# A graph layer with attention as host for its messages: layer changes, gather lead and the b2 add rearranged

## Chip, cores and metric

One Trainium2 chip, one core. The metric is the device time of one execution in microseconds (us), the median of several runs. All data is fp32.

## What is computed

One layer of a graph transformer on 3125 nodes of 256 features and 100,000 directed edges with three attributes each: a graph convolution and a four-layer transformer over the same normalized nodes, added, then a mixture of experts. Cut to what matters:

```
xn = layernorm(x)
# graph convolution
m   = concat([xn[src], edge_attr], 1)
h_N = segment_sum(relu(m @ W1.T + b1), dst, N)
h   = relu(concat([xn, h_N], 1) @ W2.T);  h = h / max(norm(h), 1e-12)
# transformer, 4 layers, 8 heads, no mask
for i in range(4):
    z = layernorm(y) * g1[i] + c1[i]
    q = softmax(z @ Wq[i] * s, over the head's 32 features)
    k = softmax(z @ Wk[i] * s, over the nodes)
    y = y + (q @ (k.T @ (z @ Wv[i])) per head) @ Wo[i] + bo[i]
    z = layernorm(y) * g2[i] + c2[i]
    y = y + gelu(z @ W1[i] + b1[i]) @ W2[i] + b2[i]
x = x + h + y
# 16 experts, the two best of each node, their shares by softmax
x = x + layernorm(moe(layernorm(x)) + layernorm(x)) * gamma + beta
```

## The kernel before

The nodes lie in 25 tiles of 125. The transformer takes them in seven blocks (`BLOCKS`) of 4, 4, 4, 4, 4, 3 and 2 tiles, numbered 0 to 6; blocks of more than two tiles are worked in pairs of tiles.

**Engines and order.** Instructions of PE, ACT and POOL go out in the order in which the code stands; so do those of DVE inside the `manual_schedule` blocks. Elsewhere a scheduler arranges DVE.

**Messages.** The message product over node features is done once per node (`proj`, in DRAM). `load_chunk` (L338) gathers 128 rows of `proj` by an indirect DMA from POOL's queue. Eight chunks make a group, of which there are 98; a group's rows lie in two of six `gat` buffers, and its edge attributes come by SP's queue into one of two `ea` buffers. `message_step` (L383) multiplies the attributes by their weights on PE (`pw`), adds the product to the gathered rows on DVE (L397), applies relu on ACT (L398) and builds a one-hot matrix `hot` on DVE (L400). A group later, `sum_step` (L358) runs `sum_pq` (L372), 16 products of `hot` and `gat` into `pq` and a copy to `osb` on ACT (L381), and, for the group before that, `sum_win` (L362): two transposes of `osb` and four adds into `hNT` on DVE.

**Where they run.** The groups are spread as filler through layers 0 to 2. The list `due` (L407) gives each step a place, in groups: a chunk of group g at g + 0.125 (j + 1) - LEAD for its j-th (from 0), with LEAD 1.25; the sum step at g; the message step at g + 0.5. `worked` (L426) is called by each stage of the transformer with the columns that it put on PE, moves `place` on by a share of the total, and issues the steps that have come due. Ahead of the first gather of such a call POOL copies one element of what the stage made (`tick`, L436), so that gathers can't run ahead of the transformer. `held` keeps `worked` from issuing anything; `only_loads` limits it to gathers.

**A layer.** For each block b the loop (L860) does: first FFN product with gelu (`stage_f1`); exponential keys and q transposed (`stage_ek`, `stage_qT`) and the key-value product (`stage_m`) of the next layer's block b - 2; attention output (`stage_y`) of block b + 1; the transposed first norm (`stage_t1`) of block b - 1; second norm (`stage_ln2`) of b + 1; the second FFN product (`stage_f2`); keys and q (`stage_k`, `stage_q`) of b - 1 for the next layer; and so on. `stage_ln2` also adds b2 to the block's residual, by `add_b2` (L714), on POOL.

**The layer change.** `stage_m` sums keys times values over all blocks (`msum`), rescaled when the running maximum of the keys grows; so the next attention output can't begin before the last block's keys are done. After the last second FFN product come k and q of block 5, its `ek`, `hT` of block 6, halves of m of block 5 with k of block 6 between them, q transposes of 5, `ek` of 6 and m of 6. `context` (L642) then divides by the key sums (`mean`), starts the last block's q, transposes (`meanT`), multiplies by Wv (`ctx`, kept per head in `ctxT`) and Wo (`mo`), with the shares of the last q between. Its argument `between` lists what PE is given at three points. After it the y products start. Message steps run here too: `fill(2)` (L440) issues one message step after the last FFN product, `fill_win` (L448) starts one sum step after `ek` of block 6, and the rest of it (`sum_pq`) is given to `context` or, at the change to the last layer, runs at once where there is one.

**After the messages.** From 1604 us the last layer runs without them, with the products of the graph convolution (`stage_g`, called `h` in the convolution's formula) as filler in its context and b2 added block by block; the experts follow.

Of the kernel before, what the change touches and what calls it, by code (L numbers as in the profile page):

```python
# [8 lines left out]
F32 = mybir.dt.float32  # L9
# [8 lines left out]
D = 256  # L18
P = 128
TP = 125  # L20
# [5 lines left out]
NG = (NCH + G - 1) // G  # L26
# [13 lines left out]
BT = 4  # L40
# [25 lines left out]
def gps_layer(ctx: ExitStack, tc: tile.TileContext, a, out):  # L66
# [153 lines left out]
    with ExitStack() as ph:  # L220
# [205 lines left out]
        def worked(columns, mark=None):  # L426
# [6 lines left out]
            while due and due[-1][0] <= place and not (only_loads and due[-1][1]):  # L433
# [158 lines left out]
        def q_shares(pair, qf):  # L592
# [49 lines left out]
        def context(l, between):  # L642
# [60 lines left out]

        def stage_ln2(b, adder=nc.gpsimd):
            r = BLOCKS[b]
            finish_stats(r)
            xh = tmp.tile([TP, BT, D], F32, name="xh")
            st["xh", b] = xh
            for i, t in enumerate(r):
                normalize(xh[:, i, :], xm[:, t, :], t)  # L710
            if adder is not None:
                add_b2(b, adder)

        def add_b2(b, adder=nc.gpsimd):  # L714
            r = BLOCKS[b]
            xs = xm[:, r[0]:r[-1] + 1, :]
            adder.tensor_add(xs, xs, b2[:TP, None, :].to_broadcast([TP, len(r), D]))
# [86 lines left out]

        rest = None
        in_order = {mybir.EngineType.PE, mybir.EngineType.Activation, mybir.EngineType.Pool}
        last = DEPTH - 1
        with tc.manual_schedule(engines=in_order):

# [7 lines left out]
            for b in range(NB):  # L817
# [3 lines left out]
                if b < NB - 1:  # L821
                    stage_q(0, b)
                else:
                    held = True
                if b > 1:
# [19 lines left out]
            stage_m(0, NB - 1)  # L845
            for l in range(last):
                start_layer(l)
                with tc.manual_schedule(engines={mybir.EngineType.DVE}):
                    if l == 0:
                        context(l, [lambda: stage_qT(l, NB - 2, slice(0, 1)),  # L850
                                    lambda: stage_qT(l, NB - 2, slice(1, 2)), lambda: None])
                    else:
                        context(l, [lambda: None, lambda: None, rest])
                    load(l + 1, "Wk", "Wq", "Wv")
                    (y00, y01), (y10, y11), (y20, y21) = [pairs(b) for b in range(3)]
                    y_added(*y_products(y00))
                    held, only_loads = False, True
                    y_added(*y_products(y01))
                    stage_ln2(0, None)
# [5 lines left out]
                    y21 = y_products(y21)  # L865
                    for y in (y11, y20, y21):
                        y_added(*y)
                    only_loads = False
                for b in range(NB):
# [12 lines left out]
                    if b + 1 < NB:  # L882
                        stage_ln2(b + 1)
                    stage_f2(l, b)
                    stage_stats(b)
# [6 lines left out]
                    if b + 1 < NB:  # L892
                        stage_t2(l, b + 1)
                    if b > 0:
                        stage_q(l + 1, b - 1)
                    if b < NB - 1:
                        stage_ln1(b)
                stage_ek(l + 1, NB - 2)
                stage_t1(l + 1, NB - 1)
                stage_m(l + 1, NB - 2, [0])  # L900
                stage_k(l + 1, NB - 1)
                stage_m(l + 1, NB - 2, [1])
                stage_qT(l + 1, NB - 2)
                stage_ek(l + 1, NB - 1)
                rest = fill_win()
                if l + 1 == last:
                    rest()
                stage_m(l + 1, NB - 1)
            while due:
                _, _, step, i = due.pop()  # L910
                step(i)
# [296 lines left out]
        with tc.manual_schedule(engines=in_order - {mybir.EngineType.Pool}):  # L1208
# [7 lines left out]
            with tc.manual_schedule(engines={mybir.EngineType.DVE}):  # L1216
                context(last, [lambda: stage_g(0, slice(0, 1)), lambda: stage_g(0, slice(1, 2)),
                               lambda: stage_qT(last, NB - 1)])
# [279 lines left out]
```

## Time and profile before

The median of five runs is 2163.39 us (2153.59 to 2173.75).

| | |
|---|---|
| profiled execution, its time | 2163.46 us |
| its span | 2161.8 us |
| mean granted clock of PE over the span | 0.932 |
| first and last message add on DVE (L397) | 161.5 and 1551.4 us |
| last second FFN product to first y product, layer 0 to 1 | 602.98 to 635.73 us |
| the same, 1 to 2 | 1091.22 to 1123.58 us |
| the same, 2 to 3 | 1571.05 to 1603.65 us |
| gathers on POOL (L348) | 784, 969 ns each, 760.1 us busy |

The profile is of one execution. PE is TensorE's products, PEld its weight loads, DVE VectorE, ACT ScalarE, POOL GpSimd; a queue that starts DMAs has a q behind its engine's name. A line such as `L397 DVE TENSOR_TENSOR gat<-gat,pw` names the code line, the engine, the operation, what is written and what is read. "idle before" is the time for which an engine did nothing ahead of an instruction, and the name after the arrow is what ended it, where the profile can tell: "issue" means nothing that it shows, "remote" an event of another queue. The granted clock is the part of full speed at which PE was let run.

### The profile page before, as it was taken

To read this page: it belongs to the slowest core of one execution; us is meant where nothing else is said; L and a number is where in the kernel's file an instruction comes from. 1 tells how busy PE (TensorE), PEld (TensorE's weight loads), DVE (VectorE), ACT (ScalarE), POOL (GpSimd) and SP (SyncE) were. 2 spreads that over 40 slices of the span, in tenths; PEclk is the share of its full clock that TensorE was granted. 3 is DMA by queue.
4 is the path that set the end of the run, shared out by engine and by line. 5 is a ranking of instruction groups with operands and counts; after the bars stand their busy time and mean duration, and the time that the engine had idled before them with its cause. 6 is when DMAs were issued, how large, how long until landed. Compare 5 with 4: busy or idle time off the path is not lost. (4 is left out here: it accounts for less than half of the span.)

```text
span 2161.8 us, 28580 instructions
## 1 busy us (share of the span) xinstructions
PE 1916.7 (89%) x8965; PEld 1262.8 (58%) x8965; DVE 1167.3 (54%) x3729; ACT 748.5 (35%) x1352; POOL 1110.8 (51%) x1404
## 2 busy tenths in 40 slices
PE   6997998898888989898888998898889999899984
PEld 4774554554564554555564454555676777778761
DVE  8654454645565455555565546555565566533335
ACT  3532334334323344344433334343422222222222
POOL 1016666666627666566626656666303335655431
PEclk9998999998888989898999989999999999999997
DMA  6122222232322222223322222332222101477846
GB/s 180 58 68 84 85 78 86 76 86 82 100 82 83 81 83 86 74 84 87 109 85 79 83 75 79 86 86 81 73 81 73 42 18 29 131 265 269 275 170 178
DMA packets 95088, 216.64 MB, mean 100 GB/s; under 512 B 26760, under 2 KB 53391, under 8 KB 90192
## 3 DMA queue, kind: packets, MB, share of 16 engines
q0 software_dynamic: 45904, 121.36, 19.5%
q1 hardware_dynamic: 49024, 93.34, 13.5%
q8 instruction: 77, 1.26, 0.2%
q14 instruction: 83, 0.68, 0.1%
HBM read 192.20 MB, written 22.35 MB: 99 GB/s over the span
## 5 line engine op out<-in xcount | busy, mean ns | idle before, releaser
L348 POOL DMA_INDIRECT gat<-proj,src_i x784 | 760.1, 969 | 229.1 <-issue 188.6
L745 PE MATMUL f_ps<-ww,gT 128*125 128x256 f32 x1600 | 378.9, 391 | 14.5 <-issue 9.1
L735 PE MATMUL f_ps<-h2T,ww 128*128 128x500 f32 (+2 forms) x896 | 376.8, 570 | 16.7 <-ACT h2T L459 6.6
L745 PEld LDWEIGHTS f_ps<-ww,gT 128*125 128x125 f32 x1600 | 300.5, 192 | 93.9 <-issue 33.9
L397 DVE TENSOR_TENSOR gat<-gat,pw 128x512 f32<-128x512 f32 x392 | 251.9, 678 | 153.6 <-PE pw L392 91.4
L398 ACT ACTIVATE gat<-gat 128x512 f32<-128x512 f32 x392 | 238.4, 630 | 276.7 <-DVE gat L397 183.6
L735 PEld LDWEIGHTS f_ps<-h2T,ww 128*128 128x128 f32 x896 | 172.2, 199 | 200.1 <-issue 138.7
L737 ACT ACTIVATE gT<-f_ps,ffb 128x500 f32<-128x500 f32 (+2 forms) x224 | 135.9, 631 | 139.2 <-PE f_ps L735 108.1
L392 PE MATMUL pw<-w1w,ea 8*128 8x512 f32 x784 | 147.2, 662 | 32.6 <-issue 5.8
L378 PE MATMUL pq<-gat,hot 128*32 128x256 f32 x1568 | 149.2, 399 | 30.1 <-ACT gat L398 20.2
L370 DVE TENSOR_TENSOR hNT<-hNT,win_ps 128x64 f32 x392 | 84.8, 216 | 132.7 <-remote 45.7
L381 ACT COPY osb<-pq 128x256 f32<-128x256 f32 x98 | 36.5, 372 | 324.1 <-remote 149.7
L400 DVE TENSOR_TENSOR hot<-slot,drel 128x256 f32<-128x256 f32 x98 | 49.0, 500 | 157.5 <-remote 58.2
L688 PE MATMUL y_ps<-mo,qT 128*125 128x256 f32 x400 | 107.3, 418 | 11.7 <-issue 5.0
L576 PE MATMUL q_ps<-wwq,hT 128*125 128x256 f32 x400 | 107.0, 423 | 9.7 <-DVE gat L397 7.8
L1201 POOL DMA_INDIRECT slots<-rec,at x50 | 59.5, 1189 | 105.5 <-DVE rs_u L115 63.7
L750 DVE TENSOR_TENSOR xm<-xm,f_ps 125x512 f32<-125x512 f32 (+1 forms) x52 | 34.6, 666 | 139.2 <-PE f_ps L745 69.0
L629 PE MATMUL m_ps<-xh,ek 125*128 125x257 f32 x400 | 101.2, 402 | 9.5 <-issue 5.2
L378 PEld LDWEIGHTS pq<-gat,hot 128*32 128x32 f32 x1568 | 52.2, 111 | 95.8 <-issue 43.5
L552 PE MATMUL k_ps<-hT,wwk 128*128 128x500 f32 (+2 forms) x224 | 102.1, 604 | 5.1 <-DVE hT L461 4.4
L576 PEld LDWEIGHTS q_ps<-wwq,hT 128*125 128x125 f32 x400 | 82.5, 212 | 36.4 <-DVE gat L397 10.8
L688 PEld LDWEIGHTS y_ps<-mo,qT 128*125 128x125 f32 x400 | 80.4, 207 | 37.0 <-issue 11.6
(270 smaller groups left out, 2673.6 us busy)
## 6 DMA issues: line engine op xcount, KB each, us to landing
ew<-ffn_w SPq DMA_DIRECT2D x33, 1154.0 KB
gat<-proj,src_i POOLq DMA_INDIRECT x784
ww<-mix_W SPq DMA_DIRECT2D x8, 1024.0 KB
ea<-ea_g SPq DMA_DIRECT2D x98, 64.0 KB
hNT<-ffn_w SPq DMA_DIRECT2D x4, 1154.0 KB
ogs<-outs SPq DMA_DIRECT2D x10, 448.0 KB
xnT_d<-stage SPq DMA_DIRECT2D x5, 500.0 KB
xnT<-xnT_d SPq DMA_DIRECT2D x5, 500.0 KB
```

Of the source, the lines that this page charges most:

```text
L348: nc.gpsimd.indirect_dma_start(out=gats[-1][:, (j // SC) % 2, j % SC, :], out_offset=None, in_=proj, in_offset=bass.IndirectOffsetOnAxis(a ...
L378: nc.tensor.matmul(pq[s * W:(s + 1) * W, :], hot[:, s * SC + i, :], gats[s // 2][:, s % 2, i, :], start=(i == 0), stop=(i == SC - 1))
L392: nc.tensor.matmul(pws[s], ea[s * W:s * W + SC * 4, :], w1w[s * W:s * W + SC * 4, :], start=True, stop=True)
L397: nc.vector.tensor_add(msg, msg, pws[s])
L398: nc.scalar.activation(msg, msg, AF.Relu)
L552: nc.tensor.matmul(ps, wt["Wk"][:, h, c * P:(c + 1) * P], hT[:, h, :m], start=(h == 0), stop=(h == KC - 1))
L576: nc.tensor.matmul(ps[:, i, :], st["hT", b][:, c, cols(o + i)], wt["Wq"][:, c, :], start=(c == 0), stop=(c == KC - 1))
L629: nc.tensor.matmul(ps, st["ek", b][:, i, c * P:(c + 1) * P], xh1s[b % 2][:, i, :], start=(i == 0), stop=(i == n - 1))
L688: nc.tensor.matmul(ps[:, i, :], qT[:, c, cols(t0 + i)], mo[:, c, :], start=(c == 0), stop=(c == KC - 1))
L735: nc.tensor.matmul(ps, wt["W1"][:, c, f * P:(f + 1) * P], st["h2T", b][:, c, :m], start=(c == 0), stop=(c == KC - 1))
L737: nc.scalar.activation(gT[:, f, :m], ps, AF.Gelu, bias=ffb[:, l, f:f + 1])
L745: nc.tensor.matmul(ps[:, i, :], st["gT", b][:, f, cols(o + i)], wt["W2"][:, f, :], start=(f == 0), stop=(f == NF - 1))
```

## The change

- LEAD goes from 1.25 to 1.5: gathers and loads of attributes are issued a quarter of a group earlier.
- The sum step of group g is due at g + 0.15 instead of g. The message step stays at g + 0.5.
- `fill` and its call are gone, so no message step is issued in a layer change. `fill_win` and the rest of its sum step are offered in `context` for layers 1 and 2 alone, between `meanT` and `ctx` and between `ctx` and `mo`; in the instructions as built it finds no sum step to start there.
- The last block's q is made ahead of m of that block, by the new `last_q`, in a buffer of the tag "xh"; the shares stay in `context`. The q transposes of block 5 move to the start of `context`, ahead of `meanT`; those of block 6 from between the y products to the end of `context`. The four lists of `between` are called at four points instead of three.
- In the layer change, k of block 5 now stands ahead of the first norm of block 6; the shares of block 5 stand after both of its exponentials.
- DVE's order is that of the code from the statistics of the last block through the y products of the next layer, where before it was so from `context` on.
- b2 is added on DVE in layers 0 to 2 (7 adds a layer, 21 in all). In the last layer it stays on POOL, except for the one that was on DVE before.

```diff
-        LEAD = 1.25
+        LEAD = 1.5
         due = [(c / G + 1 / G - LEAD, 0, load_chunk, c) for c in range(NCP)]
-        due += [(g, 1, sum_step, g) for g in range(1, NG + 2)]
+        due += [(g + 0.15, 1, sum_step, g) for g in range(1, NG + 2)]
         due += [(g + 0.5, 2, message_step, g) for g in range(NG)]
...
-        def fill(kind):
-
-            while due and due[-1][1] in (0, kind):
-                _, k, step, i = due.pop()
-                step(i)
-                if k == kind:
-                    return
...
+        def last_q(b):
+
+            st["qs", b] = tmp.tile([TP, BT, D], F32, tag="xh", name="qs")
+            pair, = pairs(b)
+            st["q", b] = pair, q_exp(b, pair, q_products(b, pair))[0]
...
             for c in range(KC):
                 nc.vector.tensor_scalar(mean[:, c, :], msum[:, c, :D], ksr[:, c:c + 1], None, op0=ALU.mult)
-
-            b = NB - 1
-            pair, = pairs(b)
-            st["qs", b] = tmp.tile([TP, BT, D], F32, name="qs")
-            q_ps = q_products(b, pair)
+            between[0]()
...
             affine(meanT, ps, l, 0)
-            qf, _ = q_exp(b, pair, q_ps)
-            between[0]()
+            between[1]()
...
             nc.vector.tensor_mul(ctxT, ps, bmask[:, None, :].to_broadcast([P, KC, P]))
-            q_shares(pair, qf)
-            between[1]()
+            q_shares(*st["q", NB - 1])
+            between[2]()
...
-            between[2]()
+            between[3]()
...
-        def stage_ln2(b, adder=nc.gpsimd):
+        def stage_ln2(b, adder=nc.vector):
...
-        def add_b2(b, adder=nc.gpsimd):
+        def add_b2(b, adder=nc.vector):
...
+                context(l, [lambda: stage_qT(l, NB - 2), sums_begun, lambda: rest[0](),
+                            lambda: stage_qT(l, NB - 1)])
...
-                    y10, y11 = y_products(y10), y_products(y11)
-                    stage_qT(l, NB - 1)
-                    y20 = y_products(y20)
-                    y_added(*y10)
-                    stage_t2(l, 0)
...
+                y10, y11, y20 = y_products(y10), y_products(y11), y_products(y20)
+                y_added(*y10)
+                stage_t2(l, 0)
...
+                dve.close()
...
-                    if b == NB - 1:
-                        stage_ln1(b)
-                        held = True
-                        fill(2)
...
+                held = True
+                dve = dve_in_order()
+                stage_stats(NB - 1)
+                stage_k(l + 1, NB - 2)
+                stage_ln1(NB - 1)
+                st["qs", NB - 2] = tmp.tile([TP, BT, D], F32, name="qs")
+                two = [(pair, q_products(NB - 2, pair)) for pair in pairs(NB - 2)]
+                qfs = [(two[0][0], q_exp(NB - 2, *two[0])[0])]
                 stage_ek(l + 1, NB - 2)
                 stage_t1(l + 1, NB - 1)
+                qfs += [(two[1][0], q_exp(NB - 2, *two[1])[0])]
+                for pair_qf in qfs:
+                    q_shares(*pair_qf)
                 stage_m(l + 1, NB - 2, [0])
                 stage_k(l + 1, NB - 1)
+                last_q(NB - 1)
+                stage_ek(l + 1, NB - 1)
                 stage_m(l + 1, NB - 2, [1])
-                stage_qT(l + 1, NB - 2)
-                stage_ek(l + 1, NB - 1)
-                rest = fill_win()
-                if l + 1 == last:
-                    rest()
                 stage_m(l + 1, NB - 1)
+            dve.close()
...
-                        add_b2(0)
+                        add_b2(0, nc.gpsimd)
```

More of the change, by code (lines that the diff above doesn't have):

```diff
@@ L803, in start_layer, with dve_in_order @@
             nc.sync.dma_start(b2, rows_bcast(a["mix_b2"][l], P))
-        rest = None
         in_order = {mybir.EngineType.PE, mybir.EngineType.Activation, mybir.EngineType.Pool}
         last = DEPTH - 1
+        def dve_in_order():
+            stack = ExitStack()
+            stack.enter_context(tc.manual_schedule(engines={mybir.EngineType.DVE}))
+            return stack
         with tc.manual_schedule(engines=in_order):
@@ L823, in gps_layer @@
                 else:
+                    last_q(b)
                     held = True
@@ L846, in gps_layer, with sums_begun @@
             for l in range(last):
+                if l == 0:
+                    dve = dve_in_order()
                 start_layer(l)
[L848 to L859, printed above, removed]
-                    y10, y11 = y_products(y10), y_products(y11)
-                    stage_qT(l, NB - 1)
-                    y20 = y_products(y20)
-                    y_added(*y10)
-                    stage_t2(l, 0)
[L865 to L868, printed above, removed]
+                rest = [lambda: None]
+                def sums_begun():
+                    if l > 0:
+                        rest[0] = fill_win()
+                context(l, [lambda: stage_qT(l, NB - 2), sums_begun, lambda: rest[0](),
+                            lambda: stage_qT(l, NB - 1)])
+                load(l + 1, "Wk", "Wq", "Wv")
+                (y00, y01), (y10, y11), (y20, y21) = [pairs(b) for b in range(3)]
+                y_added(*y_products(y00))
+                held, only_loads = False, True
+                y_added(*y_products(y01))
+                stage_ln2(0, None)
+                y10, y11, y20 = y_products(y10), y_products(y11), y_products(y20)
+                y_added(*y10)
+                stage_t2(l, 0)
+                y21 = y_products(y21)
+                for y in (y11, y20, y21):
+                    y_added(*y)
+                only_loads = False
+                dve.close()
                 for b in range(NB):
@@ L884, in gps_layer @@
                     stage_f2(l, b)
+                    if b == NB - 1:
+                        break
                     stage_stats(b)
[L886 to L889 removed]
                     if b > 0:
                         stage_k(l + 1, b - 1)
[L892 to L893 removed]
+                    stage_t2(l, b + 1)
                     if b > 0:
                         stage_q(l + 1, b - 1)
[L896 to L897 removed]
+                    stage_ln1(b)
+                held = True
+                dve = dve_in_order()
+                stage_stats(NB - 1)
[4 more added lines that the diff above has]
+                qfs = [(two[0][0], q_exp(NB - 2, *two[0])[0])]
                 stage_ek(l + 1, NB - 2)
                 stage_t1(l + 1, NB - 1)
+                qfs += [(two[1][0], q_exp(NB - 2, *two[1])[0])]
+                for pair_qf in qfs:
+                    q_shares(*pair_qf)
                 stage_m(l + 1, NB - 2, [0])
                 stage_k(l + 1, NB - 1)
+                last_q(NB - 1)
+                stage_ek(l + 1, NB - 1)
                 stage_m(l + 1, NB - 2, [1])
[L903 to L907 removed]
                 stage_m(l + 1, NB - 1)
+            dve.close()
             while due:
@@ L1216, in gps_layer @@
             with tc.manual_schedule(engines={mybir.EngineType.DVE}):
-                context(last, [lambda: stage_g(0, slice(0, 1)), lambda: stage_g(0, slice(1, 2)),
-                               lambda: stage_qT(last, NB - 1)])
+                context(last, [lambda: stage_qT(last, NB - 2), lambda: stage_g(0, slice(0, 1)),
+                               lambda: stage_g(0, slice(1, 2)), lambda: stage_qT(last, NB - 1)])
                 stage_y(last, 0)
```

## The prediction

> **What bounds the kernel now.** I read the totals and slices first, then a table of stretches, then the list of waits, then the timeline of one layer change.
>
> The totals and slices give the engine that sets the end:
>
> ```profile
> PE 1916.7 (89%) x8965; PEld 1262.8 (58%) x8965; DVE 1167.3 (54%) x3729; ACT 748.5 (35%) x1352; POOL 1110.8 (51%) x1404
> ...
> PE   6997998898888989898888998898889999899984
> ...
> PEclk9998999998888989898999989999999999999997
> ```
>
> PE is busy 89% of 2161.8 us, and its slices fall to 8 only where DVE, ACT and POOL work too; there the granted clock falls as well. The stretches say how much this is (columns after the length: busy time of PE, weight load, DVE, ACT, POOL; granted clock; DMA share; GB/s). The first three are the steady parts of layers 0, 1 and 2, the next three the changes of layer, the last is layer 3 after the messages:
>
> ```profile
> 145.00:602.00 457.00, 396.83 (x1926) 237.91 (x1925) 238.26 (x716) 169.67 (x296) 296.75 (x405) 0.91 0.29 83
> 636.00:1092.00 456.00, 409.41 (x1958) 241.52 (x1961) 242.53 (x727) 173.20 (x301) 293.65 (x397) 0.92 0.29 84
> 1124.00:1570.00 446.00, 399.93 (x1908) 237.46 (x1907) 242.71 (x714) 167.45 (x292) 266.37 (x359) 0.93 0.27 78
> 602.98:636.00 33.02, 25.83 (x119) 18.98 (x120) 22.21 (x65) 11.26 (x23) 7.68 (x9) 0.84 0.34 97
> 1092.00:1124.00 32.00, 25.50 (x129) 18.44 (x121) 22.11 (x69) 11.34 (x23) 9.80 (x11) 0.89 0.37 110
> 1570.00:1604.00 34.00, 27.98 (x135) 22.93 (x134) 20.12 (x69) 9.79 (x20) 0.00 (x0) 1.00 0.37 113
> 1604.00:1822.00 218.00, 218.00 (x925) 164.63 (x924) 132.72 (x591) 57.25 (x88) 72.32 (x55) 1.00 0.15 39
> ```
>
> Without messages PE is full at clock 1.00. In the steady parts it idles 60.2 + 46.6 + 46.1 = 153 us, and the missing 9, 8 and 7% of clock are worth at most 41 + 36 + 31 = 108 us: some 0.7 us of lost clock beside each idle us. Idle time of PE in the steady parts is thus what can be won, and the waits between 145 and 1570 us name it (sum, times, longest, in us):
>
> ```profile
> ACT gat L398 <- DMA gat<-proj,src_i: 27.2, 13, 6.4
> PE pq L378 <- ACT gat L398: 20.2, 18, 2.6
> DVE gat L397 <- DMA gat<-proj,src_i: 17.9, 8, 5.5
> ```
>
> PE's largest single wait is that of the sums `pq` for the relu of the messages of their own group; the messages themselves wait for gathered rows. PE's waits for `gat` on DVE, ahead of second-norm transposes, q products and window transposes, are 8.2 + 7.8 + 3.9 = 19.9 us more. A change of layer looks like this (start, length, engine, what; in brackets the idle time before):
>
> ```profile
> 610.36 0.54 DVE L554 TENSOR_REDUCE here<-k_ps 128x1 f32<-128x375 f32 x1
> ...
> 611.75 0.54 DVE L554 TENSOR_REDUCE here<-k_ps 128x1 f32<-128x375 f32 x1
> ```
> ```profile
> 613.36 1.89 PE L614 MATMUL ek_ps<-ident,ekT 128*125 128x128 f32 x6 [3.99 <-ACT ekT L563]
> ```
>
> The message adds and the rsqrt steps stand ahead of and between the two maxima of the keys; PE waits 3.99 us for the exponentials, and from 612.3 to 622.5 its clock is 0.50.
>
> **Part 1: layer changes, A = -2 us.** From the last FFN product to the first y product they take 32.75, 32.36 and 32.60 us. Message steps fill 2.59 us of PE in the first (window transposes, sums, edge products) and 3.97 in the second; these move to the steady part at the same PE cost, so the net changes are 30.16 and 28.39. After the change: the wait of 3.06 us for the exponentials in the second goes (four message adds of 0.68 left DVE ahead of the maxima); m of the last block comes to wait some 1.85 us, since in the order by hand DVE reaches its keys' maxima only after the shares of two pairs of q (1.00 + 0.32 + 1.03 = 2.35 us in the second change, of which I let 0.5 lie beside other work); and the last block's q transposes (0.59) move ahead of y. 28.39 - 3.06 + 1.85 + 0.59 = 27.8, for the first and second change: -2.4 and -0.6. At 2-3, where no message step runs and no wait exceeds 1.6 us, only the additions apply: +2.4. The q transposes leave the y phase twice (-1.2); the first context gains 0.4, as the last q is ready before it. Sum -2.2, taken as -2. Bounds: if none of the added waits appears and the half clock of the first change (8.46 us of work at 0.5, 4.2 lost) goes too, -12; if DVE's order written by hand waits at each step for ACT as it does once for `meanT` (1.43 us in the second change), some six more steps across three changes make +8. The gathers that were pulled in there are issued later, with the others; they cost POOL 0.97 us each wherever they run.
>
> **Part 2: sums 0.15 group later, B = -10.** Groups follow each other every 14.3 us (first message add at 161.5, last at 1551.4, 97 intervals): 0.15 is 2.15 us. That is over the mean of the 18 waits of `pq`, 20.2 / 18 = 1.12, and just under the longest, 2.6. All 20.2 us could go; but PE then meets the next late result earlier, so I take half. Bounds 0 and -20.2. Late next are `osb` and the window transposes of the same sum, which follow a group later and so have cover.
>
> **Part 3: gathers 0.25 group earlier, C = -5.** 3.6 us against waits for gathered rows of up to 5.5 and 6.4, 45.1 in all. Only what reaches PE counts: 19.9 us for `gat` on DVE; I take a quarter, since those adds also wait for `pw` (91.4 us on DVE). Bounds 0 and -18. The cost: `gat` has six buffers, three groups. The first gather of group g is due at g - 1.125 and comes to g - 1.375; the sums that free its buffer, those of g - 3, were due at g - 2 and come to g - 1.85. The slack shrinks from 0.875 to 0.475 group, 12.5 to 6.8 us. On POOL's queue all later gathers and the `tick` copies are behind a gather that waits; for `ea` on SP's queue, with two buffers freed by the edge products, it shrinks from 0.375 to 0.125 group, 1.8 us, with later loads behind it.
>
> **Part 4: b2 on DVE, D = +3.** The rows:
>
> ```profile
> L717 POOL TENSOR_TENSOR xm<-xm,b x27: 1277/2357/2382, 184.7 to 1795.1; 125x1024 f32<-125x1024 f32 x20, 125x768 f32<-125x768 f32 x4, 125x512 f32<-125x512 f32 x3
> ```
> ```profile
> L1423 DVE TENSOR_TENSOR ogs<-ogs,gamma 125x1024 f32<-125x1024 f32 x5 | 6.1, 1225 | 1.0 <-ACT ogs L1418 1.0
> ```
> ```profile
> L400 DVE TENSOR_TENSOR hot<-slot,drel x98: 390/425/3094, 122.4 to 1536.0; 128x256 f32<-128x256 f32 x98
> ```
>
> On DVE a layer's adds take 5 x 1.225 + 0.95 (768 columns, between the rows) + 0.69 (its one row of 512) = 7.77 us, 23.3 in three layers. DVE is 53% busy there, so I let its idle half hide 12; behind each add on DVE's queue stand message adds, FFN evictions and `finish_stats`, for which PE waits, so 11 are left. Back come 7.7 us, what four `hot` comparisons of 2.2 to 3.1 us took above their 0.42 beside L717 on POOL. 11 - 8 = +3. Bounds: 0 and, with the cover gone, +23.3. POOL is relieved of some 45 us, which it need not have: the page has it 51% busy.
>
> The Trainium skill, GPSIMD Engine Reference, section 1 (Specifications), has GpSimd and VectorE share their SBUF interfaces, with contention for DVE instructions with two SBUF inputs; the b2 add is one, and it now runs beside gathers issued by POOL, which speaks against this part. The trace shows the contention beside the POOL add (`hot`, 3.09 us for 0.42), but not beside gathers: the shares of q, with two SBUF inputs too, never take over 695 ns in 52. If the rule held there as beside L717, 21 adds at seven times their price would cost 23.3 x 6 = 140 us more; by the row nothing.
>
> **Part 5: clock, E = -4.** A to D take -2 - 10 - 5 + 3 = -14 of idle time from PE; at 0.7 that would bring -10. The waits that go are short, 1 to 3 us, where the throttle shown above followed 3.99, so I take -4, 0.3 for each us (0 to -10).
>
> **Sum.** -2 - 10 - 5 + 3 - 4 = -18, against the profiled execution's 2163.46 (span 2161.8, 1.7 around it), 0.07 above the median 2163.39: 2145.5, forecast 2146.
>
> **Rivals.** First: nothing measurable. The sums' waits only move to the next product, since the groups' pace is set by DVE and ACT; A and D remain, 2163.5 - 2 + 3 = 2164. For it: 183.6 us of ACT's idle time ends with DVE's message adds. Against: `pq` waits on that relu directly, and a wait shorter than the delay can't stay. Second: slower, DVE becomes the bound. Place: the FFN of each steady part, where a b2 add ahead of an eviction holds the PSUM that PE needs. All 23.3 us exposed, no gain from B and C, and 0.3 of it more by the clock as in part 5 (7): 2163.5 - 2 + 30 = 2192. It decides once over half of the adds' time is exposed and B fails. For it: PE's waits ended by DVE between 145 and 1570 us come to some 56 us already. Against: DVE is idle 47% of the steady parts, and PE's other 97 us of idle time there are not ended by it. Third: the earlier gathers find no free buffers, since POOL waits for the sums three groups back, which became later; then C is lost, 2151. For it: `osb` copies that come up to 10.5 us after their sums, more than 6.8 of slack.
>
> **How the numbers follow.** Forecast 0.50 (own range 2130 to 2160), nothing measurable 0.22, DVE the bound 0.18, no free buffers 0.10. A measurement here tells 0.5% from no change: 10.8 us, so faster is below 2152.6, slower above 2174.2. Faster: 0.42 of the forecast, 0.06 of the third rival, 0.02 of the first: 0.50. Slower: 0.17 of the second, 0.03 of the first: 0.20. Same: 0.30. The range takes most of the second rival's lower half and, below, B and C near their full bounds with D at 3: 2163.5 - 2 - 20 - 18 + 3 - 10 = 2116; 2115 to 2182.
>
> **What would show it.** Right, step by step: the wait of `pq` for the relu falls below 8 us; waits for gathered rows fall below 20; L717 is on DVE near 1.2 us in layers 0 to 2, and no `hot` exceeds 1 us beside it; the clock stays at 1.00 in the layer changes, which last 27 to 29 us; the steady parts get shorter by 4 to 6 us each. Wrong: PE's waits for DVE rise above 56 us, POOL waits for `pq` ahead of gathers, or the clock in the steady parts falls below 0.91.

## The result, and the profile after

The change makes the kernel a little slower: 2171.19 us (median of 52 runs) against 2163.72 (94 runs), a ratio of 1.0023 with a 95% interval of [1.0011, 1.0035]. The medians are of all runs; the ratio is of the fast runs alone, which leaves out the slowest few of the changed kernel's. The profiled execution took 2174.56 us, its span 2172.8, granted clock 0.924. In a later session the ratio was 1.0053 [1.0030, 1.0075] (e9). The sessions of the experiments lie at two levels, the kernel before at 2141 to 2163 us in three and at 1905 to 1909 in two, one chip having been at both; so ratios are compared within a session, and each is given with its level.

The stretches of the changed kernel, from first y product to last second FFN product and on to the next y product (length; busy time of PE, weight load, DVE, ACT, POOL; clock; DMA share; GB/s):

```profile
141.56:592.85 451.29, 404.76 (x1915) 239.74 (x1914) 243.82 (x719) 170.53 (x296) 285.21 (x404) 0.91 0.30 86
592.85:629.60 36.75, 27.49 (x115) 19.88 (x113) 19.99 (x60) 8.55 (x18) 5.73 (x7) 0.76 0.24 75
629.60:1092.10 462.50, 411.27 (x1960) 243.70 (x1959) 248.40 (x736) 171.24 (x301) 278.32 (x389) 0.90 0.29 83
1092.10:1125.72 33.62, 28.17 (x123) 18.95 (x123) 22.68 (x65) 11.45 (x23) 6.42 (x8) 0.90 0.30 88
1125.72:1571.97 446.25, 396.15 (x1935) 240.08 (x1935) 243.86 (x726) 172.00 (x298) 258.18 (x357) 0.92 0.28 80
1571.97:1608.61 36.64, 28.93 (x131) 22.97 (x129) 20.95 (x71) 8.71 (x19) 0.00 (x0) 0.95 0.34 103
```

The changes of layer take 36.75, 33.62 and 36.64 us, where they took 32.75, 32.36 and 32.60 with message steps in two of them. The steady parts add up to 1360 us; before, cut at the same events, to 1364. So in these two profiles the changes grew by 9 us although 6.6 us of PE work left them, and the steady parts fell by 4 although they took that work over. The other 7 us of the longer span lie in the last layer (263.7 us against 256.7 to its last FFN product), which varies between runs: 259.8 in e9, 256.0 in e1.

One profile doesn't place a few us, though. The changed kernel's second profile (e9) has steady parts of 1341 us in all, and changes of 34.50, 33.04 and 36.87. With the layer change of before, the first took 32.75, 33.13 and 40.24 us and the second 32.36, 41.06 and 29.00 (before, e12, e2). Only the change 2 to 3, which has no message steps, repeats: 32.60, 32.60 and 32.64 in those three, against 36.64, 36.54, 36.28 and 36.87 with the new order (changed, e1, e3, e9; 39.96 in e4). Its 4 us are the firm reading.

The waits between 145 and 1580 us (sum, times, longest), the last line from the kernel before:

```profile
PE f_ps L738 <- issue: 25.9, 48, 1.3
...
PE pq L378 <- ACT gat L398: 10.6, 11, 3.2
...
ACT gat L398 <- DMA gat<-proj,src_i: 6.2, 7, 2.0
DVE gat L397 <- DMA gat<-proj,src_i: 4.4, 2, 2.5
...
PE f_ps L745 <- issue: 9.1, 17, 1.7
```

The waits that the edits aimed at did fall: rows gathered too late cost 10.6 us instead of 45.1, relu ahead of the sums 10.6 instead of 20.2. But PE now has gaps of 25.9 us inside the second FFN product (9.1 before). The rows of the moved add and of the comparison beside it (min/median/max in ns):

```profile
L710 DVE TENSOR_TENSOR xm<-xm,b x22: 682/1216/1226, 151.7 to 1832.3; 125x1024 f32<-125x1024 f32 x15, 125x512 f32<-125x512 f32 x4, 125x768 f32<-125x768 f32 x3
```
```profile
L400 DVE TENSOR_TENSOR hot<-slot,drel x98: 391/423/490, 122.2 to 1541.2; 128x256 f32<-128x256 f32 x98
```

They are as worked out: 1.22 us on DVE, and no comparison over 0.49 us. DVE is busy for 1183.1 us instead of 1167.3, 15.8 more, close to 23.3 less the 7.7 of the slowed comparisons.

Two places in the layer changes matter. At 2 to 3, where no message step runs, DVE in its order by hand:

```profile
1582.07 0.54 DVE L453 TENSOR_SCALAR hT<-hT_ps,lnp 128x250 f32<-128x250 f32 x1 [1.97 <-ACT hT L451]
...
1585.61 0.43 DVE L589 TENSOR_TENSOR qs<-qs,qr 125x256 f32<-125x256 f32 x1
...
1587.31 0.17 DVE L551 TENSOR_SCALAR neg<-kmax 128x2 f32<-128x2 f32 x1
```

and in the kernel before:

```profile
1580.53 0.42 DVE L597 TENSOR_TENSOR qs<-qs,qr 125x256 f32<-125x256 f32 x1
1580.87 0.53 DVE L461 TENSOR_SCALAR hT<-hT_ps,lnp 128x250 f32<-128x250 f32 x1
...
1584.03 0.17 DVE L559 TENSOR_SCALAR neg<-kmax 128x2 f32<-128x2 f32 x1
```

Before, the scheduler let DVE do all q work of block 5 while ACT got ready for `hT`. In the order by hand DVE stands 1.97 us before `hT`, with the second q pair and all shares queued behind it, and the last maxima of the keys are ready 15.3 us after the last FFN product instead of 13.0. PE hardly waits for these maxima, though (PE, changed kernel):

```profile
1581.36 2.94 PE L627 MATMUL m_ps<-xh,ek 125*128 125x257 f32 x6 [1.98 <-ACT ek L613]
...
1588.10 0.95 PE L612 MATMUL ek_ps<-ident,ekT 128*125 128x128 f32 x4 [0.18 <-ACT ekT L555]
```

Its longest wait is an earlier one, of m of block 5 for `ek`, 1.98 us where it was 1.62 before. From 1581.4 to 1584.5, right behind it, the granted clock is 0.50, and the six products of m take 2.94 us instead of 1.57.

At 0 to 1 (DVE, ACT, POOL and PE of the changed kernel):

```profile
600.55 0.43 DVE L400 TENSOR_TENSOR hot<-slot,drel 128x256 f32<-128x256 f32 x1 [5.50 <-remote]
```
```profile
600.61 0.37 ACT L381 COPY osb<-pq 128x256 f32<-128x256 f32 x1 [8.26 <-remote]
```
```profile
599.39 0.95 POOL L348 DMA_INDIRECT gat<-proj,src_i  x1 [0.30 <-issue]
```
```profile
604.06 1.89 PE L612 MATMUL ek_ps<-ident,ekT 128*125 128x128 f32 x6 [4.70 <-ACT ekT L555]
```

A sum was issued just ahead of the change. Its products are recorded until 594.05, but ACT and DVE, which wait for them, go on at 600.6, when the train of gathers on POOL ends. The key maxima stand behind them on DVE and begin at 602.00, and PE waits 4.70 us, longer than the 3.99 before. In e9 it is the same, with 4.43 us. The sum alone doesn't do it: e4, e11 and e17 have one at the same place, but with no gather running beside it; there the transposes of the keys begin 6.4 us after the last FFN product instead of 11.2, and the change takes 27.0 to 30.0 us.

### The profile page after: what moved, and what is told of

Same layout as the page of the kernel before. It is cut to its first block, busy times and chain, and to the rows that moved or that the text cites. A ratio compares the mean times of both kernels' runs of the same rounds, so it can differ in the third digit from the quotient of the medians.

```text
span 2172.8 us, 28537 instructions
## 1 busy us (share of the span) xinstructions
PE 1927.9 (89%) x8965; PEld 1270.2 (58%) x8965; DVE 1183.1 (54%) x3750; ACT 747.9 (34%) x1352; POOL 1069.9 (49%) x1386
## 5 line engine op out<-in xcount | busy, mean ns | idle before, releaser
L738 PE MATMUL f_ps<-ww,gT 128*125 128x256 f32 x1600 | 403.7, 406 | 34.5 <-issue 28.1
L728 PE MATMUL f_ps<-h2T,ww 128*128 128x500 f32 (+2 forms) x896 | 371.2, 562 | 23.1 <-ACT h2T L451 10.7
L738 PEld LDWEIGHTS f_ps<-ww,gT 128*125 128x125 f32 x1600 | 312.9, 200 | 129.1 <-issue 69.8
L378 PE MATMUL pq<-gat,hot 128*32 128x256 f32 x1568 | 137.9, 397 | 23.3 <-issue 11.0
L400 DVE TENSOR_TENSOR hot<-slot,drel 128x256 f32<-128x256 f32 x98 | 41.2, 421 | 121.9 <-remote 49.1
L681 PE MATMUL y_ps<-mo,qT 128*125 128x256 f32 x400 | 98.3, 398 | 4.0 <-issue 3.2
L204 PE MATMUL e_ps<-ew,hs 128*128 128x256 f32 x400 | 97.2, 380 | 0.5 <-DVE o L208 0.3
L627 PEld LDWEIGHTS m_ps<-xh,ek 125*128 125x128 f32 x400 | 77.8, 199 | 32.3 <-ACT ek L613 13.2
```

The source lines that it names most:

```text
L378: nc.tensor.matmul(pq[s * W:(s + 1) * W, :], hot[:, s * SC + i, :], gats[s // 2][:, s % 2, i, :], start=(i == 0), stop=(i == SC - 1))
L627: nc.tensor.matmul(ps, st["ek", b][:, i, c * P:(c + 1) * P], xh1s[b % 2][:, i, :], start=(i == 0), stop=(i == n - 1))
L681: nc.tensor.matmul(ps[:, i, :], qT[:, c, cols(t0 + i)], mo[:, c, :], start=(c == 0), stop=(c == KC - 1))
L728: nc.tensor.matmul(ps, wt["W1"][:, c, f * P:(f + 1) * P], st["h2T", b][:, c, :m], start=(c == 0), stop=(c == KC - 1))
L738: nc.tensor.matmul(ps[:, i, :], st["gT", b][:, f, cols(o + i)], wt["W2"][:, f, :], start=(f == 0), stop=(f == NF - 1))
```

## Experiments

Each was timed in five rounds beside the kernel before. Theory 1 put the loss in the layer change, theory 2 in the steady parts; the others came with the readings. The upper level is the one near 2150 us, the lower that near 1907.

**e1, e2: the two halves of the change.** e1 is the changed kernel with these lines as before; e2 the kernel before with them as after (and with POOL named in the last layer's own call of `add_b2`, as in the change).

```diff
-        LEAD = 1.25
+        LEAD = 1.5
-        due += [(g, 1, sum_step, g) for g in range(1, NG + 2)]
+        due += [(g + 0.15, 1, sum_step, g) for g in range(1, NG + 2)]
-        def stage_ln2(b, adder=nc.gpsimd):
+        def stage_ln2(b, adder=nc.vector):
-        def add_b2(b, adder=nc.gpsimd):
+        def add_b2(b, adder=nc.vector):
```

> The changed kernel with LEAD 1.25, the sums due at g and b2 on POOL, as before: only the layer change and DVE's order there are new. Theory 1 (the layer change is where the time is lost: 36.75, 33.62 and 36.63 us against 32.75, 32.36 and 32.60 in the profiles, 9.3 us more, of which 3 to 6.6 come back in the steady parts as message work): 3 to 7 us slower than before, ratio 1.0015 to 1.0035, layer changes of 33 to 37 us. Theory 2 (the loss is in the steady parts, by b2 on DVE and by sums that now meet the second FFN product): ratio 0.998 to 1.000.

> The kernel before with LEAD 1.5, the sums due at g + 0.15 and the 21 b2 adds on DVE; the layer change is that of before. Theory 1 (the layer change loses): ratio 0.996 to 0.999, waits for gathered rows below 15 us as in the changed kernel. Theory 2 (these edits lose): ratio 1.002 to 1.005.

Level 2163: e1 1.0041 [1.0014, 1.0069], e2 0.9946 [0.9912, 0.9980]. By the times theory 1 stands: the new layer change loses some 9 us (3 to 15), the three other edits win some 12 (4 to 19). Theory 2 falls. The profile of e1 bears theory 1 out only in part: its changes take 28.61, 31.13 and 36.54 us, and 33 to 37 was expected of all three; in e2 the last takes 32.64. The 4 us of 2 to 3 and the 6.6 us of message work that moves to the steady parts, less the 5.4 by which the first two are shorter, make 5 of the 9. The two halves multiply to 0.9987, below the 1.0023 of the whole; their intervals leave room for that, so whether they disturb each other is open.

**e3: sums at g again**, in the changed kernel.

```diff
-        due += [(g + 0.15, 1, sum_step, g) for g in range(1, NG + 2)]
+        due += [(g, 1, sum_step, g) for g in range(1, NG + 2)]
```

> The changed kernel with the sums due at g again. Theory 3 (a sum's products run slowly while POOL issues gathers, so putting them later only moves the wait from the relu into the next products): within 3 us of the changed kernel, 2166 to 2175, with PE's waits for the relu of messages back near 20 us and the gaps inside the second FFN product down from 25.9 to about 10. Forecast's term B (the later sums win 10 us): 2181.

1.0040 [1.0015, 1.0064], 2172.89 us: no different from the changed kernel, as theory 3 had it; the relu waits are back (25.0 us). The gaps in the second FFN product fell only to 19.1, not to 10.

**e4: POOL waits for each sum**, in the changed kernel.

```diff
                 nc.scalar.copy(osbs[g - 1], pq)
+                nc.gpsimd.tensor_copy(tick, osbs[g - 1][:1, :1])
```

> The changed kernel, and after each sum POOL copies one element of its result osb, so no further gather is issued until the sum's products have ended. Theory 3: the delay from the last recorded product of a sum to the copy of its result, 299 us over 98 groups in the changed kernel (10.7 at most), falls below 100 us, as gathers no longer run beside most sums; the gaps inside the second FFN product (25.9) shrink below 12; the time falls by 5 to 30 us, 2140 to 2166. Rival (the delay has nothing to do with gathers): it stays near 300, and POOL's waiting makes the kernel the same or slower, 2170 to 2190.

0.9895 [0.9862, 0.9927], 2139.61 us, the fastest of e1 to e4 and just below the 2140 to 2166 expected; the reason given for it is not borne out. The delay from a sum's last recorded product to the copy of its result stayed at 278 us over all groups (299 in the changed kernel), where below 100 was expected, since the edit doesn't keep gathers from the sums: those issued ahead of POOL's wait still run beside 86 of the 98 sums (79 in the changed kernel). The gaps in the second FFN product halved, to 13.2. What wins here is open.

**e5, e6: two parts of the layer change undone**, in the changed kernel. e5 puts the last q back behind `mean`; e6 lets ACT copy `ek` ahead of the exponential of q.

```diff
-            between[0]()
+            b = NB - 1
+            pair, = pairs(b)
+            st["qs", b] = tmp.tile([TP, BT, D], F32, tag="xh", name="qs")
+            q_ps = q_products(b, pair)
...
             affine(meanT, ps, l, 0)
+            between[0]()
+            st["q", b] = pair, q_exp(b, pair, q_ps)[0]
             between[1]()
...
-                    last_q(b)
...
-                last_q(NB - 1)
```
```diff
-                qfs = [(two[0][0], q_exp(NB - 2, *two[0])[0])]
                 stage_ek(l + 1, NB - 2)
+                qfs = [(two[0][0], q_exp(NB - 2, *two[0])[0])]
```

> The changed kernel with the last block's q products back in the context, between mean and meanT, and the q transposes of block 5 between meanT and ctx. Theory 1a (q hid behind the division by the key sums; ahead of m it costs its 1.9 us of PE in each change): the change from layer 2 to 3, where no messages run, falls from 36.6 to 34 to 35 us, and the whole by about 6, ratio to before 0.998 to 1.001. Theory 1b (the loss is the order on ACT, where the exponentials of keys wait to be copied behind the exponential of q): 2 to 3 stays above 36, ratio as the changed kernel, 1.001 to 1.004.

> The changed kernel with stage_ek of block 5 ahead of the first exponential of its q, so that ACT copies ek first. Theory 1b: m's wait for ek in the change from 2 to 3 (1.98 us) falls below 0.7, the clock there stays at 1.00, and the change takes 33 to 34.5 us instead of 36.6; the whole falls by 4 to 9, ratio to before 0.998 to 1.001. Theory 1a: the change stays above 35.5, ratio 1.001 to 1.004.

Level 1909, where the changed kernel itself has no run: 0.9958 [0.9939, 0.9977] and 0.9952 [0.9935, 0.9968]. So these ratios can't be set against it. The 2 to 3 change took 35.53 and 36.48 us. Neither theory holds alone. In e6 the wait of m for `ek` is gone, as expected, but the transposes of the last keys then wait 2.17 us; in e5 they wait 1.93. Both times PE then waits for the last key maxima: with either edit DVE's chain is the next limit, and this led to theory 1c.

**e9, e10, e11: DVE's order in the layer change left to the scheduler.** e9 is the changed kernel; e10 fixes DVE's order from `context` on only; e11 is e10 with the edit of e5.

```diff
-                if l == 0:
-                    dve = dve_in_order()
+                dve = dve_in_order()
...
                 held = True
-                dve = dve_in_order()
                 stage_stats(NB - 1)
...
-            dve.close()
```

> The changed kernel itself, to stand beside the next ones on the same chip: the earlier call ran on a chip on which the kernel before takes 1909 us instead of 2163, and held no run of the changed kernel. If this chip is of the first sort: 1.0023 of before, 2 to 3 in 36.6 us.

> The changed kernel with DVE's order by hand from context on only, as before; in the layer change the scheduler arranges DVE again. Theory 1c (the order by hand makes DVE wait 1.97 us for hT with the second q pair and the shares, 2.9 us, behind it, so the maxima of the last keys come at T + 15.3 instead of T + 12.3): the maxima of block 6 come at T + 12 to 13 us, and the change from 2 to 3 falls from 36.6 to 34 to 35 us, the products of q (1.9) left on the path; the whole 4 to 8 us below e9. Rival (it is the q products alone): 2 to 3 stays above 36.

> e10, and the last q back in the context as in e5, where it alone brought the change from 36.6 to 35.5 since the path moved to DVE. If order and q are the two causes together: 2 to 3 takes 32 to 33 us, as before, and the whole is 8 to 14 us below e9, about 0.996 of before on the first sort of chip. If another cause is left: above 34 us.

Level 2148: e9 1.0053 [1.0030, 1.0075], e10 1.0001 [0.9977, 1.0024], e11 0.9992 [0.9973, 1.0010]. In e10 DVE at 2 to 3:

```profile
1571.18 0.53 DVE L453 TENSOR_SCALAR hT<-hT_ps,lnp 128x250 f32<-128x250 f32 x1
...
1573.99 0.17 DVE L551 TENSOR_SCALAR neg<-kmax 128x2 f32<-128x2 f32 x1
```

No wait stands before `hT`, the maxima are ready 12.0 us after the last FFN product (at 1561.97) instead of 15.3, m no longer waits for the first `ek`, and the clock stays at 1.00. The 2 to 3 change takes 36.87, 33.69 and 32.19 us in the three. So theory 1c is shown for this change, with the q products as the smaller second cause. Over the whole kernel the ratio falls by 0.0052 from e9 to e10, 11 us, more than the 4 to 8 expected and uncertain by some 7; the three changes of the profile give 5.4 of them. The further 0.0009 to e11 is within the noise: 13 us in all, of 8 to 14 expected.

**e8, e12: b2 on DVE alone**, in the kernel before, at both levels.

```diff
-        def stage_ln2(b, adder=nc.gpsimd):
+        def stage_ln2(b, adder=nc.vector):
-        def add_b2(b, adder=nc.gpsimd):
+        def add_b2(b, adder=nc.vector):
-                        add_b2(0)
+                        add_b2(0, nc.gpsimd)
```

> The kernel before with the 21 b2 adds of layers 0 to 2 on DVE and nothing else changed. Forecast's term D: +3 us, ratio 1.000 to 1.003. Rival: POOL's queue is free for gathers and the slowed hot comparisons (2.2 to 3.1 us) are gone, while DVE's 23.3 us hide wholly: 0.996 to 0.999.

> The kernel before with the 21 b2 adds on DVE alone, as e8 (0.9946 there). Forecast's term D was +3 us: 1.000 to 1.003. If b2 on DVE wins here too: 0.993 to 0.997, and then it alone accounts for the 0.9946 of e2, with nothing left for the later sums and earlier gathers.

0.9946 [0.9927, 0.9964] at level 1909, 0.9950 [0.9919, 0.9982] at 2148: a gain of 10 to 11 us at both. The forecast's term falls, and at the upper level this edit alone gives what e2 gave with all three, although waits for gathered rows are still 32.9 us in e12 and only 4.0 in e2.

**e15: the POOL work put back beside it.** POOL adds b2 to itself, with no one waiting for the result.

```diff
             adder.tensor_add(xs, xs, b2[:TP, None, :].to_broadcast([TP, len(r), D]))
+            if adder is nc.vector:
+                extra = tmp.tile([TP, D], F32, name="extra")
+                for _ in r:
+                    nc.gpsimd.tensor_add(extra, b2[:TP, :], b2[:TP, :])
```

> e12 (b2 on DVE), and at each of these places POOL adds b2 to itself into a scratch row, once for each tile of the block: the same columns on POOL as before the move, with no one waiting for them. Theory 6 (b2 on DVE wins because POOL's adds held up the gathers behind them and slowed DVE beside them): the gain goes, 0.998 to 1.002, and some hot comparisons take over 1 us again. Rival (it wins because the add on DVE no longer makes DVE and POOL wait for each other): 0.993 to 0.997 as e12.

Level 1905: 1.0050 [1.0037, 1.0064], 1% above e8, which is of another session. The gain is gone and more. The waits for gathered rows up to 1310 us, first of e15, then of e8:

```profile
DVE gat L397 <- DMA gat<-proj,src_i: 30.1, 20, 5.7
ACT gat L398 <- DMA gat<-proj,src_i: 25.3, 11, 8.3
```
```profile
ACT gat L398 <- DMA gat<-proj,src_i: 11.2, 7, 4.9
DVE gat L397 <- DMA gat<-proj,src_i: 8.8, 6, 3.0
```

55.4 us against 20.0, while the slowest `hot` took 0.81 us, where some over 1 were expected, and DVE was busy for 1182.9 us against 1181.8. So POOL's queue alone is enough to take the gain away. Whether the 7.7 us of slowed comparisons, which e8 and e12 end as well, have a share in it was not tried. The kernel before shows how the queue is held up (POOL):

```profile
677.21 0.95 POOL L348 DMA_INDIRECT gat<-proj,src_i  x1 [0.30 <-issue]
678.16 4.70 POOL L717 TENSOR_TENSOR xm<-xm,b 125x1024 f32<-125x1024 f32 x2
683.03 0.96 POOL L348 DMA_INDIRECT gat<-proj,src_i  x1 [0.16 <-issue]
```

Two adds stood in the middle of a train of gathers and held it up for 4.7 us.

**e13: later sums and earlier gathers alone**, in the kernel before (the first four lines of the diff of e1).

> The kernel before with LEAD 1.5 and the sums at g + 0.15; b2 stays on POOL, the layer change is that of before. Forecast's terms B and C: 15 us less, 0.993. Theory 4 (the waits they end, 45 us for gathered rows and 20 of the sums, are not what sets PE's pace; PE's signals leave late while gathers are issued, whatever the places): 0.998 to 1.002, although waits for gathered rows fall below 15 us.

Level 1905: 0.9950 [0.9937, 0.9964], 9.5 us won, against theory 4 and two thirds of the forecast's 15. Waits for gathered rows, expected below 15 us, are still 38.8: with POOL's adds between the gathers, the earlier place alone doesn't end them. At the upper level there is only e2 beside e12, 0.9946 and 0.9950 in different sessions, which leaves nothing for these two edits, with some 0.4% of room.

**e14, e17, e18: message steps back in the layer change.** e17 is the kernel of e11; e14 and e18 are that kernel with `fill` and its call again:

```diff
                 held = True
                 stage_stats(NB - 1)
+                fill(2)
```

> e11 with fill(2) back, so that a message step, and with it the sum step in context, runs in the changes 0 to 1 and 1 to 2 again. Theory 5 (the steps filled PE's idle time of some 7 us in each change, and cost 6.6 us of PE in the steady parts when they are moved there): 0.3 to 0.5% below e11, 0.994 to 0.997 of before. Rival (the steps' late signals delay the maxima of the keys as much): as e11, 0.998 to 1.001.

> The kernel of e11 again (the changed kernel with DVE scheduled in the layer change and the last q in the context; no message steps there), as the pair of e18 on the same chip. On the first sort of chip 0.997 to 1.001; on the faster one, by theory 5, 0.992 to 0.995.

> The kernel of e14 again (e17 with the message steps in the layer change). Theory 5 (the steps fill idle time of PE in the change): 0.3 to 0.5% below e17. Rival (their late signals cost as much): equal to e17 within 0.2%.

e14, level 1905: 0.9894 [0.9879, 0.9909], below what either theory expected. If gains multiply, b2 and the two other edits without any new layer change would give 0.9946 x 0.9950 = 0.9896, so at this level nothing would be lost in that layer change any more. At level 2141, e17 1.0024 [1.0000, 1.0048] and e18 1.0040 [1.0014, 1.0066]: no gain from the steps. Theory 5 falls there. The changes of e17, without steps:

```profile
586.55:613.59 27.04, 21.01 (x115) 15.60 (x113) 19.20 (x60) 8.37 (x18) 4.95 (x6) 1.00 0.35 99
1063.16:1096.66 33.50, 25.96 (x124) 18.63 (x123) 22.08 (x65) 11.23 (x23) 6.55 (x8) 0.90 0.30 89
1541.73:1573.93 32.20, 26.47 (x131) 21.69 (x128) 19.89 (x71) 8.58 (x19) 0.00 (x0) 1.00 0.41 117
```

The first is as short as 27.04 us, yet the second takes 33.50 at clock 0.90. With the steps (e18) they take 35.21, 34.18 and 32.19, and the whole is the same within the noise: a longer change need not be a slower kernel.

**e7, e16: all that won, together**: e2 with the line of e4.

> The kernel before with LEAD 1.5, sums at g + 0.15, b2 on DVE (as e2) and POOL's copy of osb after each sum (as e4). If the gains of e2 (0.9946 of before) and e4 (0.9895 / 1.0023 = 0.987 of the changed kernel) are of different waits, they multiply: 0.982, 2124 us. If POOL's waiting only mends what the new layer change upset, it stays at e2: 0.992 to 0.997.

> e7's kernel (layer change of before, LEAD 1.5, sums at g + 0.15, b2 on DVE, POOL waits for each sum), which had 0.9863 on the faster chip. On a chip of the first sort: 0.980 to 0.987, below e4 (0.9895), which has the new layer change.

0.9863 [0.9842, 0.9884] at level 1909, between the two values expected, and 0.9857 [0.9842, 0.9872] at 1905, below e14 of the same session. It beats the kernel before at the lower level, where the changed kernel has no run; at the upper level it has none itself, and e4 with 0.9895 is the best that was measured there.

## Why the prediction was wrong

The forecast was 2146, faster by 18; it came to 2171, slower by 5 to 11. The time lies inside the range, on the wrong side of no change.

**Part 1, the layer change: the step that failed.** Forecast -2, measured +9 alone, with 3 to 15 possible (e1). The term that was mis-sized is DVE's order by hand. It stood in the sum as 1.85 us a change, for shares of q ahead of the last key maxima, and that DVE would wait for ACT stood in the text only as the upper bound, counted as six short waits. The runs put the order at 11 us (e9 to e10). What it does is best seen at 2 to 3, where +2.4 was forecast and +4.0 came: DVE waits once, 1.97 us for `hT` (1.91 in each of the other changes), with 2.9 us of q work behind it, and the maxima came 2.3 us later as forecast. But PE's loss did not come at m of the last block, which waits 0.73 us as before. It came at m of block 5: a wait of 1.98 us for `ek`, and 3.1 us at half clock behind it, both gone in e10. The late maxima were next in line, as e5 and e6 show. The q products were costed at nothing when moved ahead of m; behind `mean` they had hidden the division by the key sums, and ahead of it they cost 1.5 us (e10 to e11 at 2 to 3).

The stall in 0 to 1 was to go with the message adds; it grew to 4.70, with a sum just ahead of the change and a gather beside that sum; the forecast had neither. That is not the hand order's doing: e10, without that order, begins the transposes of the keys as late (12.0 us after the last FFN product) and takes 34.0, while e11 and e17, with no gather beside that sum, take 27.0. That this is near the forecast's 27.8 is luck, since the 1.85 counted there is not in it.

**Part 4, b2: wrong sign.** The price on DVE was right, 23.3 us less 7.7 (the four slowed comparisons took 1.7 to 3.1 us, not 2.2 to 3.1; their sum is right). That 11 would be exposed was not: no run shows any of it, and the edit wins. And POOL's relief was costed at nothing because POOL is 51% busy, though part 3 named the gathers queued behind its instructions. The move is worth 10 to 11 us (e8, e12), all of it lost without POOL's relief (e15). The contention of which the Trainium skill's page GPSIMD Engine Reference (section 1, Specifications) warns for two SBUF inputs did not appear beside gathers: the 22 adds, ten of them with a gather running, took at most 1226 ns.

**Parts 2 and 3, sums and gathers.** Both waits fell, the gathered rows' as stated and the sums' to 10.6 us, not below 8; the third rival did not occur (POOL's waits for `pq` ahead of gathers are 4.3 us, 2.6 before, none over 0.6). At the lower level the two edits won 9.5 of 15 us. At the upper level nothing is left of the 15 that could be measured (e2 beside e12, e3 beside the changed kernel). The step that failed here too is that a wait that ends is time that PE wins: in the profile the wait of the sums fell by 10 us and the gaps of the product that follows rose by 17. That this is because PE's signals leave late there is argued, not shown.

**Part 5** followed from the idle time that should have gone; the profile's clock fell to 0.924 instead, and over the runs it is 0.927 (median).

The first rival, nothing measurable, gave 2164 and a time within 0.5%, which is what came. Its reason holds in part, since the sums' wait did move to the next product; but its A and D were -2 and +3, and a loss and a gain of some 10 us each came. So the nearness is mostly luck. The second rival did not occur: PE's waits for DVE fell from 69 us, counted in full (the 56 of the prediction are the longest 30 rows), to 51.

**Open:** at the upper level the kernel of e11 and e17 (0.9992, 1.0024) stays about 0.5 to 0.8% above e2, of another session, with DVE's order, the q products and (e18) the message steps as before. The places of the q transposes, the q buffer shared with the second norm and the order of k and first norm remain; they were not tried singly. So some 11 of the 17 to 23 us between e2 and the changed kernel have a shown cause.

## What to carry to other kernels

An order written by hand turns each wait into a wait for all that stands behind it: before fixing it, list for every instruction that waits on another engine what is queued behind, and put independent work ahead of it. An engine that issues transfers is judged by what its other work delays, not by its busy share. And a wait that ends need not be time that is won: move one edit at a time, since a gain and a loss of the same size look like no change. And before a difference between two profiles is explained, look at a second profile of the same kernel: here the steady parts of two differ by 19 us.

## What was not expected of the hardware

At the upper level, PE's signals (by which the other engines learn that a product is done) can leave late after a sum beside which POOL issues a gather. In the changed kernel the twelve behind 592.78 are, in order, one of the window transposes, eight of the sum, two of k and one of q. They left at 593.32, 594.77, 596.22, 597.63, 597.67, 599.06, 599.10, 600.49, 600.53, 601.98, 602.04 and 602.13 us, in steps of 1.41 to 1.49 us, some two or three at a time, although the products are recorded one after another until 599.36.

From a sum's last recorded product to the copy of its result, all groups together, it is 306 us before, 299 after, at most 10.7. In the changed kernel the 79 sums beside which a gather ran have a median of 2.49 us, the 19 others 0.20, with five of these over 1 us. The clearest case is the first layer change, where many of the kernels have a sum that is recorded to end 1.2 us after the last FFN product. At the upper level the copy of its result comes 4.9 to 7.8 us after that product in the five profiles with a gather beside the sum (changed, e2, e3, e9, e10) and 1.4 us in the four without (e4, e11, e17, e18).

At the lower level the copy comes after 1.4 us in all six profiles that have this sum, each with a gather beside it, so a gather is not enough by itself. In all, e8 and e14 have 68 and 75 us there, at most 4.4, where the same kernels at the upper level (e12, e18) have 269 and 302, and their steady parts add up to 1105 and 1094 us instead of 1324 and 1337. What puts a session at one level or the other was not found; the same chip was at both.
